# In-place products in tiles of two states, and one accumulating transfer for two of them, in a state-space recurrence

## The chip, the cores and the metric

The kernel runs on 1 core of one Trainium2 chip. The metric is the time of one execution on the device in microseconds (us). Before the change it is 2311.16 us, the median of 3 runs (2310.63 to 2311.9).

The core's engines are named as in the profile: PE (TensorE's matmuls), PEld (its weight loads), DVE (VectorE), ACT (ScalarE), POOL (GpSimd) and SP (SyncE, which only issues transfers here). Each takes its own instructions in order; they wait for one another by semaphores.

## The reference, cut to what matters

A residual network of four layers on x of 4 batches x 1024 positions x 128 features, all in float32. Each layer has a sequence mixer and a feed-forward part. The change lies in the mixer of the last layer, a selective state-space recurrence over 256 channels with 16 states each:

```python
xs = silu(conv(x @ in_w.T) + conv_b)
delta = softplus(xs @ wd1.T @ wd2.T + wd2_b)
Bm, Cm = xs @ wb.T, xs @ wc.T                 # 16 values per position
def step(h, inp):
    d_l, b_l, c_l, x_l = inp
    h = jnp.exp(d_l[:, :, None] * A) * h + (d_l * x_l)[:, :, None] * b_l[:, None, :]
    y_l = jnp.einsum('ben,bn->be', h, c_l)
    return (h, y_l)
y = (ys + xs * W_D) * silu(skip) @ out_w.T
```

The feed-forward part behind it has 8 experts with 512 hidden units, each computed for every position and weighted by a gate.

## The kernel before, in words

The last layer (`l3`, L1600) works in eight halves: 4 batches, each in two halves of 512 positions. The second half of a batch (h = 1) goes on from the states at the end of the first (h = 0). The 256 channels lie as two groups of 128 partitions, so a tile of one state is 128 x 2 x 512 floats.

`l3_scan` (L1824) is a generator that yields once per state n, 16 times a half. For one state:

- SP loads row n of B and of C, broadcast to all partitions, into `bn` and `cn` (L1849, four buffers each).
- POOL multiplies `ud` (delta times x) by B into a tile `db` (L1854, four buffers).
- For each channel group, ACT takes the exponential `da` of delta times A into one of two PSUM banks (L1858), and DVE runs the recurrence along the positions with one scan, in place in `db` (L1859).
- If h is 0, ACT copies the last position of both groups, 128 x 2 elements, to `carry` (L1868), from which the scans of the second half start.
- POOL multiplies `db` by C into a tile `hc` (L1870, four buffers).
- The sum over the states is PE's: `add` (L1836) multiplies an `hc` tile by the identity, once per channel group, and accumulates in two PSUM banks, `pys`. A list `sums` holds what is still to be summed: (state, tile, the state at which it is due).
- In batches 1 to 3, after each odd state, POOL issues a transfer that adds the odd state's `hc` to the even state's (L1875, `accum_op`), so that PE sums one tile for two states. The last state of the last half is left out of this.

`l3` advances one state of the scan, one step of the sum and finish of the half before (`l3_sum` L1884, `l3_finish` L1909: gate, output product, norm, router) and one step of the preparation of the next half (`l3_prepare` L1723), all under a raised priority (L1624); then come steps of the second mixture-of-experts layer (`moe`) and three or four steps of `work`, the experts of the last layer (`l3_experts` L1647, `l3_ffn` L1967). The experts take up a half when more than three states have passed since its router (L1655, L1637). Each expert has four matmuls `ph` (L1983) with a Relu on ACT (L1985), 16 matmuls `py` (L1993), and DVE adds them to `h_acc` under the gate (L2010).

The order on each engine is not the order of the source: a scheduler (`schedule_with_timeline_sim`, L2221) plans the program with its own costs, takes the instruction with the highest priority among those that are ready by its plan, and gives out tile buffers as they come free in it. The order is then fixed.

Of the kernel before, what the change touches and what calls it, by code (L numbers as in the profile page):

```python
# [12 lines left out]
F32 = mybir.dt.float32  # L13
# [3 lines left out]
ALU = mybir.AluOpType  # L17
# [3 lines left out]
P = 128  # L21
# [21 lines left out]
E3, NST, DDELTA, KCONV = 256, 16, 64, 4  # L43
# [17 lines left out]
class Net:  # L61
# [1762 lines left out]
    def l3_scan(self, u):  # L1824


        nc, c3, b, h = self.nc, self.c3, u["b"], u["h"]
        sp, wp, aneg = c3["sp"], c3["wp"], c3["aneg"]
        wout = c3["we"][:, :, ND:]
        xnT, xs, dl, ud, rows = (u[k] for k in ("xnT", "xs", "dl", "ud", "rows"))  # L1830
        carry = wp.tile([P, 2, NST], F32, name="carry") if h == 0 else u["prev"]["carry"]
        u["carry"] = carry
        u["py"] = py = []
        u["sums"] = sums = []

        def add(n, hc):  # L1836
            if not py:
                py.extend(self.psb(f"y{ec}", [P, 512], f"pys{ec}") for ec in range(2))
                u["first"] = n
            for ec in range(2):  # L1840
                self.mm(py[ec], self.ident, hc[:, ec, :], n == u["first"], n == NST - 1)

        u["add"] = add
        for n in range(NST):
            bc = []
            for i, nm in enumerate(("bn", "cn")):
                t = wp.tile([P, 1, 512], F32, name=nm, bufs=4)
                r = i * NST + n
                nc.sync.dma_start(  # L1849
                    out=t[:, 0, :], in_=rows[r : r + 1, :].to_broadcast([P, 512])  # L1850
                )
                bc.append(t.to_broadcast([P, 2, 512]))
            db = wp.tile([P, 2, 512], F32, name="db", bufs=4)
            nc.gpsimd.tensor_mul(db, ud, bc[0])  # L1854
            for ec in range(2):
                j = ec * NST + n
                da = self.psb("da", [P, 512], "da")
                nc.scalar.activation(da, dl[:, ec, :], AF.Exp, scale=aneg[:, j : j + 1])  # L1858
                nc.vector.tensor_tensor_scan(  # L1859
                    db[:, ec, :],  # L1860
                    da,
                    db[:, ec, :],
                    carry[:, ec, n : n + 1] if h else 0.0,
                    ALU.mult,
                    ALU.add,
                )
            if h == 0:
                nc.scalar.copy(carry[:, :, n : n + 1], db[:, :, 511:512])  # L1868
            hc = wp.tile([P, 2, 512], F32, name="hc", bufs=4)
            nc.gpsimd.tensor_mul(hc, db, bc[1])  # L1870
            if n in (9, 12):
                self.l3_gate(u, n // 12)
            if n % 2 and b > 0 and not (u["final"] and n == NST - 1):
                hc0 = sums.pop()[1]
                nc.gpsimd.dma_start(out=hc0, in_=hc, accum_op=ALU.add)  # L1875
                sums.append((n, hc0, n + 2))
            else:
                sums.append((n, hc, n + 2))
            for k in range(2):
                if sums and sums[0][2] <= n:  # L1880
                    add(*sums.pop(0)[0:2])
            yield
# [342 lines left out]
```

## Time and profile before

| What | Value |
|---|---|
| median of 3 runs | 2311.16 us |
| the profiled execution's own time | 2313.25 us |
| its span | 2311.5 us |
| mean granted TensorE clock | 0.928 |
| busy share of the span: PE, DVE, ACT, POOL | 87%, 59%, 52%, 44% |
| recurrence, from its first product with B to its last sum | about 1388 to 2181 us |
| products with B (L1854): of 128, 112 under the name `ud`, mean | 2642 ns |
| products with C (L1870), 128, mean | 2499 ns |
| accumulating transfers (L1875) | 47, of 512 KB |
| matmul records of the sums (`pys`) | 324, busy 158.1 us |
| carry copies on ACT (L1868) | 64, median 194 ns |

A busy share is an average over stages. The answer by stage gives the busy time of each engine in a stretch, then the granted clock, the mean share of the 16 transfer engines in use, and GB/s. A group of instructions is read as: line, engine, operation, result<-inputs, shapes, count | busy us, mean ns of one | idle time of the engine just before them, and what ended most of it. A mean over products on POOL is longer than the 2.35 us of one alone, as a product behind an issue of a transfer is recorded from before that issue's end. A wait is read as: who waited <- for whom: us in total, times, the longest. In the timeline, "x2" is two instructions merged into one line.

### The profile page before, as it was taken

To read this page: it belongs to the slowest core of one execution; us is meant where nothing else is said; L and a number is where in the kernel's file an instruction comes from. 1 tells how busy PE (TensorE), PEld (TensorE's weight loads), DVE (VectorE), ACT (ScalarE), POOL (GpSimd) and SP (SyncE) were. 2 spreads that over 40 slices of the span, in tenths; PEclk is the share of its full clock that TensorE was granted. 3 is DMA by queue.
4 is the path that set the end of the run, shared out by engine and by line. 5 is a ranking of instruction groups with operands and counts; after the bars stand their busy time and mean duration, and the time that the engine had idled before them with its cause. 6 is when DMAs were issued, how large, how long until landed. Compare 5 with 4: busy or idle time off the path is not lost.

```text
span 2311.5 us, 46328 instructions
## 1 busy us (share of the span) xinstructions
PE 2004.4 (87%) x17788; PEld 1398.0 (60%) x17788; DVE 1355.3 (59%) x3674; ACT 1193.8 (52%) x2609; POOL 1023.8 (44%) x812
## 2 busy tenths in 40 slices
PE   6679789989999999999979865688898999898998
PEld 3455565544477777787768653346565656565666
DVE  7658544343455654654645555785777688777522
ACT  6532334322244444454555546476767786766443
POOL 5100410000123244234143337987788889888500
PEclk9768879989999999999989987899999999999999
DMA  3000110050000010031222065455775677775421
GB/s 106 0 28 10 40 38 1 19 172 0 1 3 2 3 38 22 25 89 42 77 75 79 22 203 165 123 176 169 210 220 158 172 190 198 189 190 164 117 64 51
DMA packets 138603, 211.09 MB, mean 91 GB/s; under 512 B 18644, under 2 KB 75981, under 8 KB 137998
## 3 DMA queue, kind: packets, MB, share of 16 engines
q1 hardware_dynamic: 126238, 173.87, 24.6%
q0 software_dynamic: 12144, 34.26, 7.2%
q8 instruction: 140, 2.29, 0.4%
q14 instruction: 81, 0.66, 0.1%
HBM read 160.29 MB, written 23.16 MB: 79 GB/s over the span
## 4 chain that ended last, share of the span: by engine, by line
PE 44%; DVE 12%; ACT 11%; issue 4%; another core or an unknown queue 1%; POOL 1%; DMA 1%; DVEq 0%; ACTq 0%; SPq 0%; POOLq 0%
PE py L129 8%; PE ph L129 7%; PE po L1131 5%; PE pa_m L129 5%; PE pqk L129 5%; DVE db L1859 4%; PE kp_mo L129 3%; PE pys L129 2%; PE pv L129 2%; PE pr L1201 2%; ACT da L1858 1%; PE pt L133 1%; ACT hh L1985 1%; PE kp_mo L133 1%; ACT xN L176 1%
## 5 line engine op out<-in xcount | busy, mean ns | idle before, releaser
L1064 POOL TENSOR_TENSOR qt<-r_q,sb_c_turn 128x256 f32<-128x256 f32 (+1 forms) x256 | 164.4, 662 | 455.8 <-ACT r_q L1056 451.6
L1870 POOL TENSOR_TENSOR hc<-db,cn 128x1024 f32<-128x1024 f32 x128 | 315.6, 2499 | 85.0 <-PE pys L129 34.6
L129 PEld LDWEIGHTS py<-wh,hh 128*128 128x128 f32 x2048 | 254.4, 195 | 84.4 <-issue 48.2
L1854 POOL TENSOR_TENSOR db<-ud,bn 128x1024 f32<-128x1024 f32 x112 | 288.3, 2642 | 12.7 <-issue 10.2
L129 PE MATMUL ph<-xT,wh 128*128 128x512 f32 x512 | 259.4, 624 | 26.3 <-DVE h_acc L2010 8.3
L129 PE MATMUL py<-wh,hh 128*128 128x128 f32 x2048 | 261.8, 279 | 17.0 <-ACT hh L1985 7.8
L1985 ACT ACTIVATE hh<-ph,sb_cols 128x512 f32<-128x512 f32 x256 | 170.6, 681 | 134.8 <-PE ph L129 102.1
L1122 DVE TENSOR_TENSOR a<-pa_m,sb_c_near 128x256 f32<-128x256 f32 x256 | 96.7, 419 | 210.6 <-PE pa_m L129 198.1
L1079 ACT ACTIVATE kN<-kp_mo,sb_c_trig 128x128 f32<-128x128 f32 x448 | 129.8, 371 | 131.3 <-PE kp_mo L133 122.9
L1858 ACT ACTIVATE da<-dl,aneg 128x512 f32<-128x512 f32 x224 | 153.3, 689 | 79.9 <-DVE db L1859 76.5
L129 PE MATMUL pys<-hc,sb_c_ident 128*128 128x512 f32 x324 | 158.1, 618 | 18.3 <-POOL hc L1870 15.1
L1859 DVE TENSOR_TENSOR_SCAN db<-da,carry,db 128x512 f32<-128x512 f32 x128 | 157.2, 1267 | 12.4 <-ACT da L1858 9.4
L129 PEld LDWEIGHTS ph<-xT,wh 128*128 128x128 f32 x512 | 90.3, 198 | 109.3 <-issue 55.5
L1859 DVE TENSOR_TENSOR_SCAN db<-da,db 128x512 f32<-128x512 f32 x128 | 149.5, 1206 | 9.2 <-POOL db L1854 5.2
L2010 DVE SCALAR_TENSOR_TENSOR h_acc<-py,gt,h_acc 128x128 f32<-128x128 f32 x252 | 70.9, 343 | 134.2 <-PE py L129 132.2
L129 PE MATMUL pqk<-xT,wE 128*128 128x256 f32 x512 | 136.3, 389 | 8.4 <-ACT coT L1198 4.3
L129 PEld LDWEIGHTS pys<-hc,sb_c_ident 128*128 128x128 f32 x324 | 60.7, 199 | 80.5 <-issue 57.7
L129 PEld LDWEIGHTS pqk<-xT,wE 128*128 128x128 f32 x512 | 88.6, 193 | 21.8 <-DVE cv L1041 6.6
L1198 ACT COPY coT<-pt 128x512 f32<-128x512 f32 x64 | 37.5, 586 | 117.1 <-PE pt L133 117.1
L129 PE MATMUL po<-ht,wD 128*128 128x512 f32 x192 | 93.1, 597 | 0.0
L1131 PE MATMUL po<-cv,a 128*64 128x65 f32 x2048 | 89.2, 230 | 0.0
L844 DVE TENSOR_SCALAR ht<-ph,sb_cols 128x512 f32<-128x512 f32 x48 | 35.7, 749 | 90.8 <-PE ph L129 90.6
(454 smaller groups left out, 4297.4 us busy)
## 6 DMA issues: line engine op xcount, KB each, us to landing
wx<-in_wF SPq DMA_DIRECT2D x92, 384.0 KB
bn<-rows SPq DMA_DIRECT2D x128, 256.0 KB
cn<-rows SPq DMA_DIRECT2D x128, 256.0 KB
wh<-in_wH SPq DMA_DIRECT2D x64, 512.0 KB
hc<-hc POOLq DMA_DIRECT2D x47, 512.0 KB
xrows<-zero SPq DMA_DIRECT2D x4, 1472.0 KB
xg<-xrows SPq DMA_DIRECT2D x20, 256.0 KB
yrows<-ys SPq DMA_DIRECT2D x20, 256.0 KB
```

The costliest lines, as they stand in the source:

```text
L129: return self.nc.tensor.matmul(out=out, lhsT=lhsT, rhs=rhs, start=start, stop=stop)
L133: self.nc.tensor.transpose(out, in_, self.ident[0:n, 0:n])
L1064: nc.gpsimd.tensor_mul(u["qt"][:, m, a:], u["q"][:, a:], c2["turn"][:, m, o + a : o + 2 * P])
L1079: self.nc.scalar.activation(u["kN"][:, c, m, :], pk[:, c, :], AF.Copy, scale=trig[:, k, m : m + 1])
L1122: nc.vector.tensor_mul(u["a"][:, i, :, :], pa[i], self.c2["near"][:, None, :].to_broadcast([P, 2, P]),)
L1131: self.nc.tensor.matmul(out=u["po"][self.HALF[j], i, c, :], lhsT=lhsT, rhs=rhs, start=key not in u["begun"], stop=True, skip_group_check=True,
L1854: nc.gpsimd.tensor_mul(db, ud, bc[0])
L1858: nc.scalar.activation(da, dl[:, ec, :], AF.Exp, scale=aneg[:, j : j + 1])
L1859: nc.vector.tensor_tensor_scan(db[:, ec, :], da, db[:, ec, :], carry[:, ec, n : n + 1] if h else 0.0, ALU.mult, ALU.add,)
L1870: nc.gpsimd.tensor_mul(hc, db, bc[1])
L1985: nc.scalar.activation(ht, ph, AF.Relu, bias=self.col("h_b1", i=e * NK + k))
L2010: nc.vector.scalar_tensor_tensor(acc[:, c, :], py[:, c, :], gt[:, c, e : e + 1], acc[:, c, :], ALU.mult, ALU.add,)
```

## The change

`db` becomes a view of one half of a tile `pair` that holds two states, and there are four such tiles. The product with C is taken in place in `db`, and the `hc` tiles are gone. The carry is copied by DVE instead of ACT. In batches 1 to 3, after every fourth state one transfer adds the tile of states 4q+2 and 4q+3 to the tile of 4q and 4q+1; the two sums are due three states after it. In batch 0, and for the last four states of the last half, every state is summed by itself.

```diff
-            db = wp.tile([P, 2, 512], F32, name="db", bufs=4)
+            if n % 2 == 0:
+                pair = wp.tile([P, 2, 2, 512], F32, name="db", bufs=4)
+                if n % 4 == 0:
+                    base = pair
+            db = pair[:, n % 2, :, :]
             nc.gpsimd.tensor_mul(db, ud, bc[0])
...
             if h == 0:
-                nc.scalar.copy(carry[:, :, n : n + 1], db[:, :, 511:512])
-            hc = wp.tile([P, 2, 512], F32, name="hc", bufs=4)
-            nc.gpsimd.tensor_mul(hc, db, bc[1])
+                nc.vector.tensor_copy(carry[:, :, n : n + 1], db[:, :, 511:512])
+            nc.gpsimd.tensor_mul(db, db, bc[1])
             if n in (9, 12):
                 self.l3_gate(u, n // 12)
-            if n % 2 and b > 0 and not (u["final"] and n == NST - 1):
-                hc0 = sums.pop()[1]
-                nc.gpsimd.dma_start(out=hc0, in_=hc, accum_op=ALU.add)
-                sums.append((n, hc0, n + 2))
-            else:
-                sums.append((n, hc, n + 2))
+            if b == 0 or (u["final"] and n >= NST - 4):
+                sums.append((n, db, n + 2))
+            elif n % 4 == 3:
+                nc.gpsimd.dma_start(out=base, in_=pair, accum_op=ALU.add)
+                sums.extend((n - 1 + k, base[:, k, :, :], n + 3) for k in range(2))
```

## The prediction

> **What bounds the kernel now.** I read the page first, its shares by engine and its list of groups, then busy time by stage, then the waits of the recurrence stage, then the timeline around single instructions.
>
> ```profile
> PE 2004.4 (87%) x17788; PEld 1398.0 (60%) x17788; DVE 1355.3 (59%) x3674; ACT 1193.8 (52%) x2609; POOL 1023.8 (44%) x812
> ...
> L1870 POOL TENSOR_TENSOR hc<-db,cn 128x1024 f32<-128x1024 f32 x128 | 315.6, 2499 | 85.0 <-PE pys L129 34.6
> ```
>
> POOL's 44% is an average over stages with different limits. By halves of the recurrence (columns: stretch, length, busy PE, PEld, DVE, ACT, POOL, clock) it is another engine:
>
> ```profile
> 1600.00:1699.00 99.00, 82.35 (x451) 58.21 (x452) 73.59 (x146) 72.10 (x148) 84.22 (x43) 0.98 0.73 202
> ...
> 1815.00:1907.00 92.00, 85.54 (x413) 53.85 (x411) 75.71 (x147) 77.36 (x144) 81.13 (x41) 1.00 0.71 189
> 1907.00:1996.00 89.00, 81.94 (x403) 52.60 (x403) 72.22 (x131) 63.18 (x106) 80.71 (x41) 1.00 0.71 192
> 1996.00:2093.00 97.00, 90.50 (x422) 57.12 (x420) 74.09 (x139) 66.86 (x115) 81.47 (x41) 0.97 0.68 181
> ```
>
> PE is busy for 92 to 93% of three of these halves, POOL for 84 to 91%, DVE for 74 to 82%. Four quantities close together: whichever engine gets some 15 us more per half becomes the bound. The waits between 1600 and 2185 us say who is late (waiter, releaser, us, times, longest):
>
> ```profile
> DVE h_acc L2010 <- PE py L129: 48.2, 21, 6.4
> ...
> POOL hc L1870 <- PE pys L129: 34.6, 13, 5.0
> ...
> PE ph L129 <- DVE h_acc L2010: 8.3, 9, 2.9
> ...
> PE pys L129 <- DMA hc<-hc: 3.3, 4, 1.2
> ```
>
> POOL waits for PE, to get an hc buffer back; PE waits for DVE, and hardly for a transfer. In 585 us PE is busy 531.6, so all that any change off PE can give here is the 53 us that are left.
>
> **The change, part by part.**
>
> *Transfers.* 47 become 23 (four per half instead of eight in batches 1 to 3, three in the last half). On POOL an issue holds back the next product: at 1829.79 one is issued and the next product starts at 1830.38, 0.59 us later, and the pair and issue up to 1835.00 take 5.21 us against 4.66 for two products. I call it 0.6 us. If one of 1 MB costs the same, POOL gets back 24 x 0.6 = 14 us over 550 us; if it costs double, 0.4 us. I take 14 us of POOL's time. POOL is not the fullest engine, so a third of it, **-5 us**; ends 0 and -14.
> Landing: the issue at 2068.81 released PE at 2079.49, that at 2073.13 at 2082.72, so 10.7 and 9.6 us. The page gives the software queue 7.2% of 16 engines' span for 34.26 MB: 0.072 x 2311.5 / 34.26 = 4.9 us per MB, so 2.5 us more per transfer of 1 MB; landing after 12 to 13 us. Inside a half a sum is due three states after its transfer instead of two, 17 us at 5.7 us a state: hidden. At the end of a half PE may come too early by these 2.5 us: 5 ends, 0 to +12.5; it waited 3.3 us in all so far, and one transfer stands there instead of two. I take **0**.
> The row says that PE waited 3.3 us for 47 transfers. The Trainium skill, page "DMA: Bandwidth & Descriptors", section "Anatomy of one DMA", gives each transfer about 2.0 us of fixed cost; by that rule 24 transfers fewer would be worth 48 us, were they on the path, and by the row at most 3.3. I go by the row.
>
> *In place.* Each product has the same shape, so 2.33 to 2.36 us as now. The hc buffers go; db tiles hold eight states in the bytes that held four and four. In batch 0 POOL can thus run further ahead; between 1385 and 1490 it idled 9.9 us for DVE's scans and 1.9 on issue. Ends 0 and -11.8, and I take **-3**, as most of that waits for scans, not for buffers. Later, POOL's 34.6 us of waiting for PE lose their cause, but a POOL that waits for PE is not the bound: 0, except for the last product of all, which waited 4.82 us at 2166 and starts the final chain: **-2** (ends 0 and -5). A db tile is now held until PE has summed it, so a late PE holds up a product with B, 2.35 us ahead of a scan, where it held up a product with C; with eight states that is due two states early. I take 0.
>
> *Sums.* 162 products with the identity become 164: 64 in batch 0, 5 x 16, and 20 in the last half. The trace has two records each at 0.43 us pitch: four records, **+1.7 us** of PE. They come two at a time; at the end of a half the second moves one state (5.7 us) later, and with it gate and norm. The experts take a half over only after more than three states, and that covers it; without the cover it is an idle PE of up to 5.7 us, five times: 0 to +28. I take 0.
>
> *Carry.* 64 copies of 128x2 leave ACT (0.19 us each, 12 us of 1194; its 11.0 us of waiting before them moves to the next exponential, which needs the same scan: 0) and go to DVE. Without company that is 64 x 0.17 = 11 us. But here is the row that decides. One line of the kernel, L1294, copies from SBUF to SBUF on DVE in 2 or 4 elements; it takes 0.17 us, except beside POOL (DVE, then POOL):
>
> ```profile
> 1156.89 0.25 DVE L1294 COPY tend<-tend 128x2 f32<-128x2 f32 x1
> 1157.05 0.15 DVE L1295 TENSOR_TENSOR tend<-tend 128x6 f32<-128x6 f32 x1
> 1157.23 0.59 DVE L1294 COPY tend<-tend 128x4 f32<-128x4 f32 x1
> ```
>
> ```profile
> 1156.37 1.42 POOL L1064 TENSOR_TENSOR qt<-r_q,sb_c_turn 128x256 f32<-128x256 f32 x2 [3.86 <-ACT r_q L1056]
> ```
>
> POOL's two products end at about 1157.08 and 1157.79; the copies end at 1157.14 and 1157.82. Each waited until POOL's running instruction was over. The scans do not: all 128 that start a batch take 1.19 to 1.22 us, most of them beside POOL. So the carry's copy, right behind a scan on DVE's queue, should wait for the rest of a 2.35 us product: POOL is busy 0.85 of the time, half a product is left on average, 0.85 x 1.17 = 1.0 us, and 0.17 for itself. Sixteen copies give 19 us in each half that starts a batch. Ends: 0 (all in DVE's slack), and 64 x (2.35 + 0.17) = 161 us. I take the mean, since DVE has slack: its 73.6, 75.7 and 74.1 us in the first halves of batches 1 to 3 become 92.6, 94.7 and 93.1. None of the four halves above is fuller than 93% on any engine, so at that share these last 99.6, 101.8 and 100.1 us, against 99, 92 and 97: +13. At 90%, two engines being full now, 102.9, 105.2 and 103.4: +23. Batch 0's has 59.5 of 98 us and can take it. I take **+18**. Behind the copy wait the next scans, and for them ACT's exponentials (two banks) and so its Relus, and PE. POOL's product with C now waits for the copy as well, but that is over at POOL's own border; behind it waits the next product with B. 0 to +0.2 us per copy, in POOL's slack.
>
> The rows show two copies held. The Trainium skill, page "SBUF — State Buffer", section "Who interferes with whom", says that a copy on VectorE that uses both ports and a GpSimd instruction exclude each other for the whole instruction, whichever starts first; it speaks against moving the copy. By it POOL too could lose 64 x 0.17 = 11 us (estimate), which the rows do not show; with that the sum would be at most 11 us higher.
>
> **Sum:** -5 - 3 - 2 + 1.7 + 18 = +9.7 us on the profiled execution's 2313.25 us (span 2311.5 and 1.75 around it), so 2323. That execution lies 2.1 us above the median of the runs, 2311.16; as a median I say **2321**.
>
> **Rivals.**
> 1. *Faster: the buffers were the limit.* POOL's chain paces the half (products, issue, landing, buffer back), the trace's quads of 21.8 us hold 19.9 us of POOL work, and with fewer issues and no wait for PE each of 22 quads loses 0.6 and part of 1.5 us. For it: 34.6 us of waits in 13 places. Against it: PE is full in just these quads (21.80 of 21.80 us from 1827.5). A fifth to a third of PE's 53 idle us: -11 to -18, and +1.7 for the sums: 2295 to 2302. It decides if the copies find POOL between two products, so that they cost less than 0.3 us each.
> 2. *Nothing:* the copies fit DVE's slack, POOL's gain lies behind PE: 2311 to 2314, with +1.7 from the sums.
> 3. *Slower by the transfers:* PE, in order, stands before the last sums of each half for the longer landing, and the gate comes one state later: +12.5 to +28, 2324 to 2339. For it: at 2079.49 and 2082.72 PE did stand. Against it: 1.6 us in all there.
> 4. *It doesn't do what it says:* a transfer of 1 MB is issued at twice the cost, and POOL saves nothing: the forecast without -5, 2326.
>
> **How the numbers follow.** Forecast 0.44 (with rival 4), transfers 0.10, faster 0.28, nothing 0.18. What a measurement can tell from no change is 0.2%, 4.6 us. The forecast's own range is 2307 (copies +13, POOL's whole 14 gained) to 2336 (copies +23, no gain), so 0.40 of it is slower and 0.04 within; the transfers are slower; of the faster rival 0.26 is faster and 0.02 within; of nothing 0.14 is within and 0.02 on each side. Faster 0.28, same 0.20, slower 0.52. The range over all cases is 2295, rival 1's far end, to 2348, the forecast's 2336 with 12.5 for the landings. It leaves out a gain beyond a third of PE's idle time and the copies' bound of 161 us, 2 in 10.
>
> **What would show it.** Right: the copy's group on DVE has a mean near 1.2 us, DVE's busy time in the first halves of batches 1 to 3 rises to over 90 us, these halves get longer by 1 to 13 us, and those in between don't. Wrong: a mean below 0.3 us; then rival 1 or 2. The issue's 0.6 us is read behind the 23 transfers, the landing in PE's wait for them, and the buffers in POOL's waits for PE, which must be gone from the products with C. A new wait of the products with B for PE would show that the held tiles bite.

## The result, and the profile after

The changed kernel takes **2406.7 us** (median of 4 runs, 2400.6 to 2413.0) against 2311.5 us of the kernel before on the same chip: a ratio of 1.0398, 95% interval 1.0375 to 1.0420. It is slower by 4%, 95 us; 2321 had been forecast and 2348 was the upper end. The profiled execution has a span of 2398.8 us, 87 us more than before, at a mean granted clock of 0.912 instead of 0.928. The page's line of busy time, and the groups that replace that of the product with C:

```profile
PE 2043.1 (85%) x17792; PEld 1414.6 (59%) x17792; DVE 1426.2 (59%) x3738; ACT 1191.4 (50%) x2545; POOL 1003.1 (42%) x788
...
L1873 POOL TENSOR_TENSOR db<-db,cn 128x1024 f32<-128x1024 f32 x128 | 302.2, 2373 | 105.1 <-DVE carry L1872 37.0
```

The carry's copy stands only in the full list of groups (count | busy us, mean ns):

```profile
L1872 DVE COPY carry<-db 128x2 f32<-128x2 f32 x64 | 74.6, 1165 | 1.0
```

PE has four matmul records more, and 39 us more busy time: apart from these four, the same matmuls at a lower clock. POOL is less busy than before. The four halves that the prediction showed, cut in the same way (from one half's first product with C to the next's; columns as there):

```profile
1594.00:1714.00 120.00, 96.28 (x475) 66.93 (x474) 93.40 (x168) 79.27 (x149) 81.40 (x43) 0.90 0.65 181
1839.00:1953.00 114.00, 92.76 (x422) 57.53 (x422) 90.56 (x163) 77.15 (x129) 78.58 (x38) 0.90 0.55 150
1953.00:2055.00 102.00, 89.12 (x399) 55.93 (x398) 73.53 (x136) 66.97 (x110) 76.92 (x36) 0.93 0.63 166
2055.00:2167.00 112.00, 93.59 (x404) 57.84 (x403) 83.75 (x146) 63.49 (x98) 78.48 (x38) 0.89 0.56 156
```

They were 99, 92, 89 and 97 us. The three that start a batch are longer by 21, 22 and 15 us, and their DVE is busier by 10 to 20 us; but the one in between, which copies no carry, is longer by 13 us as well. So two things happened. And no engine is full: PE has gone from 83-93% down to 80-87%, DVE stands at 72 to 79%. The waits from 1600 to 2250 us:

```profile
POOL db L1873 <- DVE carry L1872: 36.7, 10, 13.1
POOL db L1858 <- DVE ud L1818: 31.2, 3, 15.7
...
POOL db L1858 <- DMA db<-db: 22.4, 6, 4.7
...
PE ph L129 <- DVE h_acc L2012: 15.1, 9, 4.0
...
PE pys L129 <- DMA db<-db: 7.1, 4, 3.2
```

POOL's waits for PE to get a buffer back, 34.6 us before, are gone. In their place it waits for the carry's copy (the product with C now overwrites what the copy reads; but e2 below, where it overwrites nothing, has 19.1 us of this wait too), for `ud` of the next half, and for the joining transfer to give back a tile. PE waits for DVE's `h_acc` nearly twice as long as before (8.3 us).

How long one copy can be held is seen where the longest starts, on DVE and then on POOL:

```profile
1609.53 0.41 DVE L1496 SCALAR_TENSOR_TENSOR sg<-sg,ph 128x256 f32<-128x256 f32 x1
1609.86 8.30 DVE L1872 COPY carry<-db 128x2 f32<-128x2 f32 x1
1618.08 0.41 DVE L1499 SCALAR_TENSOR_TENSOR mh<-sg,ph 128x256 f32<-128x256 f32 x1
```

```profile
1608.89 2.37 POOL L1873 TENSOR_TENSOR db<-db,cn 128x1024 f32<-128x1024 f32 x1
1611.21 2.34 POOL L1858 TENSOR_TENSOR db<-ud,bn 128x1024 f32<-128x1024 f32 x1
1613.51 2.34 POOL L1873 TENSOR_TENSOR db<-db,cn 128x1024 f32<-128x1024 f32 x1
1615.80 2.33 POOL L1858 TENSOR_TENSOR db<-ud,bn 128x1024 f32<-128x1024 f32 x1
1618.30 2.35 POOL L1873 TENSOR_TENSOR db<-db,cn 128x1024 f32<-128x1024 f32 x1 [0.17 <-POOL db L1858]
```

Four products follow on one another without a gap, and the copy ends at 1618.17 in the first gap between two (1618.13 to 1618.30). Of the 64 copies 25 took less than 0.2 us; each of the other 39 ended within 0.04 us of the end of a product on POOL.

What stands behind this copy on DVE's queue is what PE and ACT wait for:

```profile
1618.55 3.78 PE L129 MATMUL po<-sb_s_e,xs 128*128 128x128 f32 x16 [8.37 <-DVE mh L1499]
```

```profile
1619.66 0.69 ACT L1862 ACTIVATE da<-dl,aneg 128x512 f32<-128x512 f32 x1 [7.75 <-DVE db L1863]
```

PE sat idle for 8.37 us until `mh`, the instruction right behind the copy, and ACT for 7.75 us until the scan behind that.

### The profile page after: what moved, and what is told of

Read it like the earlier page. It is cut to its first block, busy times and chain, and to the rows that moved or that the text cites. A ratio compares the mean times of both kernels' runs of the same rounds, so it can differ in the third digit from the quotient of the medians.

```text
span 2398.8 us, 46140 instructions
## 1 busy us (share of the span) xinstructions
PE 2043.1 (85%) x17792; PEld 1414.6 (59%) x17792; DVE 1426.2 (59%) x3738; ACT 1191.4 (50%) x2545; POOL 1003.1 (42%) x788
## 5 line engine op out<-in xcount | busy, mean ns | idle before, releaser
L1873 POOL TENSOR_TENSOR db<-db,cn 128x1024 f32<-128x1024 f32 x128 | 302.2, 2373 | 105.1 <-DVE carry L1872 37.0
L129 PE MATMUL ph<-xT,wh 128*128 128x512 f32 x512 | 269.6, 642 | 49.7 <-DVE h_acc L2012 15.1
L1858 POOL TENSOR_TENSOR db<-ud,bn 128x1024 f32<-128x1024 f32 x112 | 262.5, 2363 | 71.9 <-DVE ud L1818 31.2
L129 PE MATMUL pys<-db,sb_c_ident 128*128 128x512 f32 x328 | 165.6, 645 | 26.6 <-POOL db L1873 16.3
L129 PEld LDWEIGHTS pys<-db,sb_c_ident 128*128 128x128 f32 x328 | 63.7, 206 | 99.9 <-issue 69.7
```

What stands on the lines that cost most here:

```text
L129: return self.nc.tensor.matmul(out=out, lhsT=lhsT, rhs=rhs, start=start, stop=stop)
L1873: nc.gpsimd.tensor_mul(db, db, bc[1])
```

## The experiments

Ratios are to runs of the kernel before on the same chip, with 95% intervals.

### The two parts, one at a time

**e1**: the changed kernel, carry back on ACT.

```diff
-                nc.vector.tensor_copy(carry[:, :, n : n + 1], db[:, :, 511:512])
+                nc.scalar.copy(carry[:, :, n : n + 1], db[:, :, 511:512])
```

> The changed kernel with the 64 carry copies back on ACT; nothing else differs in the source, and nothing is left out. Changed kernel 2406.7 us, kernel before 2311.5 us. Theory 1, the copies on DVE are the loss (in the trace of the changed kernel their mean is 1.17 us, and they end with POOL's instructions): 2305 to 2325 us, and PE's busy share in the six halves of batches 1 to 3 goes back from 85% to over 90%. Theory 2, the tiles are the loss (a db tile is held by the join and by PE's sums, and POOL's products with B no longer run ahead): over 2380 us, with the gaps on POOL ahead of the first product of a half as long as in the changed kernel. In between, by both: 2340 to 2370.

Measured 2350.8 us, ratio 1.0153 (1.0132 to 1.0175): in between. With the copies off DVE 56 us of the 95 are gone, and some 35 to 40 us are something else.

**e2**: the kernel before with that edit the other way round, DVE instead of ACT.

> The kernel before with one edit: the 64 carry copies on DVE. Theory 1, the copies alone are the loss: 2385 to 2410 us, with a mean copy of over 1 us. Theory 2, the tiles are the loss: 2311 to 2330 us, although the copies are as long. Both needed together: 2330 to 2350, with the first halves of batches 1 to 3 longer by some 10 us each.

2379.2 us, 1.0271 (1.0254 to 1.0288). The copies alone cost 63 us, a little under theory 1's 2385, and need nothing else of the change.

**e3**: the changed kernel with the same bytes in copies of one element.

```diff
-                nc.vector.tensor_copy(carry[:, :, n : n + 1], db[:, :, 511:512])
+                for ec in range(2):
+                    nc.vector.tensor_copy(carry[:, ec, n : n + 1], db[:, ec, 511:512])
```

> The changed kernel with each carry copy split into two DVE copies of one element per partition, one per channel group (128 instead of 64). If the copy is held by POOL only in the form that takes several elements, the mean falls from 1.17 us to about 0.16 and by theory 1 the time to 2310 to 2330 us. If any copy from SBUF to SBUF on DVE is held, the mean stays over 0.8 us, there are twice as many, and the time is 2406 or more. By theory 2 the time stays at 2380 to 2410 whatever the copies take.

```profile
L1873 DVE COPY carry<-db 128x1 f32<-128x1 f32 x128 | 15.7, 141 | 0.0
```

2356.0 us, 1.0179 (1.0146 to 1.0213). Twice as many copies take a fifth of the time: none of the 128 is held, though 91 of them run wholly inside a product on POOL. The time falls by 51 us, to about that of e1, and not to theory 1's 2310 to 2330, as the other part remains. The Trainium skill, page "VectorE: DVE Perf Modes", section "Mode 2×_2P — use both read ports for one tensor", lets a copy from SBUF to SBUF use both read ports if its outermost dimension above one is even: two elements qualify, and one element has no such dimension. That fits 1165 against 141 ns; no run here shows the ports themselves.

**e13**: the same edit as in e3 on the kernel before.

> The kernel before with the carry copied on DVE in two copies of one element per partition, 128 in all. If POOL's hold on the copy of two elements is the whole price of the 63 us: 2308 to 2325 us, with a mean copy of 0.14 us. If the move to DVE by itself, with the other order that it gives, costs a good part: 2335 to 2375.

2318.5 us, 1.0017 (1.0001 to 1.0033). Here the hold is nearly the whole price: 1.0271 with it, 1.0017 without. That another planned order made the difference can be ruled out from the traces. The copies left aside, POOL's 812 instructions follow one another in the same order in e2 and e13 (by the names of their tiles), and 3634 of DVE's 3674 and 17772 of PE's 17788 stand at the same place. For e3 and the changed kernel it is 768 of 788, 3524 of 3674 and 17614 of 17792.

The halves that start batches 1, 2 and 3, and third the one between the last two, in e13 and then in e2, cut where the last product with C ends:

```profile
1599.00:1705.00 106.00, 89.09 (x464) 60.58 (x463) 78.44 (x178) 75.34 (x142) 87.07 (x47) 0.97 0.69 193
1816.00:1913.00 97.00, 88.43 (x436) 57.15 (x435) 76.08 (x176) 74.69 (x127) 81.99 (x42) 0.98 0.67 180
1913.00:2003.00 90.00, 81.92 (x387) 51.84 (x387) 72.65 (x135) 66.02 (x110) 81.59 (x41) 0.98 0.71 191
2003.00:2093.00 90.00, 86.02 (x433) 56.71 (x432) 71.02 (x160) 62.72 (x99) 81.73 (x41) 1.00 0.73 194
```

```profile
1596.00:1721.00 125.00, 94.60 (x449) 63.78 (x448) 103.75 (x162) 74.51 (x140) 86.73 (x47) 0.89 0.59 165
1838.00:1954.00 116.00, 97.32 (x435) 62.02 (x434) 94.44 (x158) 73.94 (x124) 81.27 (x40) 0.91 0.56 150
1954.00:2044.00 90.00, 81.89 (x378) 51.44 (x378) 73.30 (x136) 66.41 (x110) 81.07 (x40) 0.96 0.71 190
2044.00:2149.00 105.00, 90.37 (x431) 58.16 (x431) 88.87 (x144) 62.78 (x99) 82.38 (x42) 0.97 0.63 167
```

The halves with copies are longer by 19, 19 and 15 us, the one without by nothing; the half in between that is not shown, of batch 1, is longer by 5. DVE is busier by 25, 18 and 18 us, and most of its idle time stays: 27.6, 20.9 and 19.0 us in e13, 21.3, 21.6 and 16.1 in e2. So the copies took little of DVE's slack; most of them was added to the length. Of batch 2's 19 us, 10 are idle PE (8.6 becomes 18.7 us) and 9 are nearly the same number of matmuls at a granted clock of 0.91 instead of 0.98. In batches 1 and 3 idle PE has more of it: 13.5 us against 5.5, and 10.7 against 4.4.

### What the tiles and the join cost

**e4**: the kernel before with the products in place alone.

```diff
-            db = wp.tile([P, 2, 512], F32, name="db", bufs=4)
+            db = wp.tile([P, 2, 512], F32, name="db", bufs=8)
...
-            hc = wp.tile([P, 2, 512], F32, name="hc", bufs=4)
-            nc.gpsimd.tensor_mul(hc, db, bc[1])
+            hc = db
+            nc.gpsimd.tensor_mul(db, db, bc[1])
```

> The kernel before with the products with C taken in place alone: db tiles of one state, eight of them, no hc tiles; carry on ACT, 47 transfers of 512 KB as before. Theory 2 in the form that holding db tiles until PE's sum costs: 2340 us or more, with POOL's products with B waiting for PE or for a transfer. Theory 2 in the form that only tiles of two states and joins over four states cost: 2300 to 2320. Theory 1: 2300 to 2315, as eight tiles in one pool let POOL run further ahead.

2333.1 us, 1.0088 (1.0056 to 1.0119): between the two forms. POOL runs on, up to eight states, and then stands at the border of the half (e4, waits from 1600 us on):

```profile
POOL db L1854 <- DVE ud L1818: 69.3, 5, 21.6
```

It was 2.5 us in the kernel before. What POOL gains inside a half it seems to lose at its end, waiting for the preparation of the next.

**e5** and **e6** asked whether that preparation paces everything: a second `next(nxt, None)` per state, in the kernel before and in e1's.

> The kernel before with one edit: two steps of the next half's preparation per state instead of one; nothing is left out. In the kernel before the first product with B of the last three halves starts 0 to 1 us after the last ud of its preparation (92, 90 and 98 us after the half's own first product). Theory A, the preparation paces the halves of every one of these kernels: ud is ready earlier, and the time falls to 2270 to 2300 us. Theory B, PE paces the kernel before (93% busy), and ud is late only because it stands in PE's order: 2305 to 2320, or slower, as the preparation is then pressed in between the sums.

> The changed kernel with the carry on ACT (2350.8 us) and two steps of the preparation per state. In it POOL waited 46 us for ud at the borders of the halves. Theory A, the in-place tiles cost time because POOL stands at the border until the preparation is over: these waits shrink to under 20 us and the time to 2300 to 2330. Theory B, it is the sums, bunched behind the joins, that hold PE up, and the wait for ud is what is left over: 2340 to 2360, with the wait only moved to another place.

2350.5 us (1.0150, 1.0118 to 1.0181) and 2373.2 (1.0257, 1.0227 to 1.0287): both slower by 22 us or more. Theory A falls: an earlier preparation does not make these kernels faster. That it pushes other work back is likely, and not shown.

**e7**: e1 with each join issued as two transfers of 512 KB.

```diff
-                nc.gpsimd.dma_start(out=base, in_=pair, accum_op=ALU.add)
+                for k in range(2):
+                    nc.gpsimd.dma_start(
+                        out=base[:, k, :, :], in_=pair[:, k, :, :], accum_op=ALU.add
+                    )
```

> The changed kernel with the carry on ACT (2350.8 us) and each joining transfer of 1 MB issued as two of 512 KB, one per state, in the same place. If the number or the size of the transfers matters by itself (one issue of 0.6 us more on POOL for each of 23; a landing that is 2 us shorter), the time moves by 5 to 15 us, up by the issues or down by the landings. If only the distance of the join matters (four states are held until the fourth product), it stays at 2346 to 2356.

2353.8 us, 1.0171 (1.0139 to 1.0203), not apart from e1: half as many transfers of twice the bytes gain nothing that can be measured.

**e8** and **e12**: e4 with six and with five tiles instead of eight (`bufs=6`, `bufs=5`).

> The kernel with in place alone (single tiles, carry on ACT, 47 transfers, 2333.1 us) with six db tiles instead of eight; the rest is as it was. If what costs is that products with B wait for tiles that PE's sums still hold, fewer tiles make it worse: 2345 to 2400. If what costs is that POOL runs too far ahead with products with B and so delays the products with C, the joins and the sums (the first sums of a half come 41 us into it instead of 32 to 36), fewer tiles make it better: 2310 to 2328.

> In place with five single tiles, carry on ACT, 47 transfers (eight tiles 2333.1 us, six 2309.2). Theory C, the fewer the better until scans wait for tiles: 2300 to 2315. Theory D, with five the products with B wait for the transfers and for PE's sums: 2325 to 2400.

2309.2 us, 0.9973 (0.9955 to 0.9991), and 2326.9, 1.0043 (1.0025 to 1.0061). With six tiles the wait for `ud` is back at 3.5 us. It is the one version ahead of both kernels, and of the kernel before by some 6 us. I took it to show that running ahead does the harm (theory C), until **e16**, with seven:

> In place with seven single tiles, carry on ACT, 47 transfers (five 2326.9 us, six 2309.2, eight 2333.1). If the time follows from how far POOL runs ahead, smoothly: 2312 to 2328. If it is the planned order that changes by chance with every edit, by some 10 to 20 us, anything from 2300 to 2345 can come, and the difference of six and eight tiles is no effect of the number.

2354.2 us, 1.0186 (1.0155 to 1.0216), the slowest of the series. Five, six, seven and eight tiles give 1.0043, 0.9973, 1.0186 and 1.0088: no order. Theory C falls too. Each edit gives the scheduler another plan (only 549 of POOL's 812 instructions stand at the same place in e4 and in e8), and the time seems to move by 1 to 2% with it; whether six tiles are a better size or a lucky plan is not told apart here.

**e9**: e1 with three tiles of two states.

> The changed kernel with the carry on ACT (2350.8 us) and three tiles of two states instead of four. Six tiles of one state had been 24 us better than eight (2309.2 against 2333.1). Theory C, eight states in flight let POOL run ahead with products with B and bunch the sums: here too it gets better, 2315 to 2340 us. Theory D, the join over four states needs its tiles (a base is held from its first product until PE's sums three states after the join, so with three tiles only one is left to go on with): worse, 2365 to 2450, with POOL's products with B waiting for PE and for the transfer.

2383.4 us, 1.0284 (1.0242 to 1.0327). Here the wait is plain:

```profile
POOL db L1858 <- DMA db<-db: 155.2, 22, 10.7
```

**e10**: e1's tiles with the join of the kernel before, 512 KB from the odd into the even half of one tile, due two states later.

```diff
-            if b == 0 or (u["final"] and n >= NST - 4):
-                sums.append((n, db, n + 2))
-            elif n % 4 == 3:
-                nc.gpsimd.dma_start(out=base, in_=pair, accum_op=ALU.add)
-                sums.extend((n - 1 + k, base[:, k, :, :], n + 3) for k in range(2))
+            if n % 2 and b > 0 and not (u["final"] and n == NST - 1):
+                hc0 = sums.pop()[1]
+                nc.gpsimd.dma_start(out=hc0, in_=db, accum_op=ALU.add)
+                sums.append((n, hc0, n + 2))
+            else:
+                sums.append((n, db, n + 2))
```

> The changed kernel with the carry on ACT (2350.8 us), its four tiles of two states kept, but the join of the kernel before: after each odd state 512 KB are added from the odd to the even half of the same tile (47 transfers), summed two states later. Single tiles with the same joins gave 2333.1 us. If what makes the 18 us between those two is the join over four states, this goes to 2325 to 2340; if it is that a tile of two states is given back as a whole, it stays at 2345 to 2365.

2326.2 us, 1.0047 (1.0027 to 1.0067): by these two runs the join over four states costs 25 us, the tiles of two states little or nothing.

**e14**: the other way round, e4's eight single tiles with the join over four, two transfers of 512 KB.

> In place in eight single tiles with the carry on ACT, joined over four states by two transfers of 512 KB after every fourth state (state 4q+2 into 4q, 4q+3 into 4q+1), sums three states later. Joined in neighbours it was 2333.1 us, and with tiles of two states and this join 2353.8. If the join over four states costs by itself, wherever the tiles end: 2345 to 2365. If it costs only because a tile of two states comes back as a whole: 2325 to 2340.

2351.1 us, 1.0165 (1.0140 to 1.0191), with the join at e1's and e7's place again.

**e15**: e1 with the last four states of each half joined in neighbours.

> The changed kernel with the carry on ACT (2350.8 us), but the last four states of each half of batches 1 to 3 joined in neighbours (odd into even, due two states later), the others over four as before; in the last half the last four are summed one by one, as they were. If the 25 us of the join over four arise at the ends of the halves (the last sums come later, and the gate, the norm and the experts behind them): 2322 to 2338. If they arise where the ninth state waits for its tile (4 to 10 us each time, once or twice a half): 2340 to 2355.

2351.1 us, 1.0173 (1.0147 to 1.0199): nothing is won by earlier sums at the end of a half. The second expectation gives the time to the ninth state's wait for its tile. There is such a wait, seen in e1 on POOL:

```profile
1843.89 0.86 POOL L1879 DMA_DIRECT2D db<-db  x1
1845.86 2.35 POOL L1873 TENSOR_TENSOR db<-db,cn 128x1024 f32<-128x1024 f32 x1 [1.11 <-DMA cn<-rows]
1848.53 0.92 POOL L1879 DMA_DIRECT2D db<-db  x1 [0.31 <-POOL db L1873]
1853.97 4.66 POOL L1858 TENSOR_TENSOR db<-ud,bn 128x1024 f32<-128x1024 f32 x2 [4.52 <-DMA db<-db]
1861.70 4.67 POOL L1858 TENSOR_TENSOR db<-ud,bn 128x1024 f32<-128x1024 f32 x2 [3.08 <-DMA db<-db]
```

The first join is issued at 1843.89, and the product with B of state 8 starts 10.1 us later; the second at 1848.53, and that of state 10 starts 13.2 us later. In the stretch of e1 from 1600 to 2200 us POOL waited so ten times, 38.3 us. But other traces do not let this wait be the cause. The same wait in e14 and in e12, from 1600 us on:

```profile
POOL db L1854 <- DMA db<-db: 1.7, 1, 1.7
```

```profile
POOL db L1854 <- DMA db<-db: 43.0, 21, 7.6
```

e14 hardly waits and is as slow as e1; e12, with joins in neighbours, waits longer than e1 and has 1.0043. So the step from "the join over four costs 25 us" to "because a tile comes back late" is not shown. Another wait, of POOL for the row of C (`cn`), was not followed up: there is none in the kernel before from 1600 us on, and it is 13.3 us in e1, 23.9 in e14, 37.8 in e7 and 41.0 in the changed kernel, but also 21.3 in e4 and 17.3 in e10, which are faster.

### The copies a third time

**e11**: e8 (six tiles) with the carry on DVE. **e17**: the same in copies of one element.

> In place with six single tiles (2309.2 us), with the 64 carry copies on DVE. On the kernel before this edit cost 63 us, on the changed kernel 56. If the copies cost some 60 us in any order of the work: 2360 to 2380. If the price hangs on how far POOL runs ahead (POOL busy behind more scans), it is under 40 here: 2330 to 2350.

> In place with six single tiles, the carry copied on DVE in two copies of one element each. Carry on ACT gave 2309.2 us, copies of two elements on DVE 2341.7. If the 32 us between them are POOL's hold on the copies: 2305 to 2320. If they come from the planned order that the move to DVE brings: 2330 to 2350.

2341.7 us, 1.0128 (1.0078 to 1.0177); and 2291.1 us on a faster chip, where the kernel before took 2278.7, so 1.0058 (1.0032 to 1.0083). Against e8's 0.9973 that is 1.5% for the copies, of which the hold makes about 0.7% (0.1 to 1.3% by the two intervals), and the other 0.85% stays when it is gone. On e11's chip 1.0058 would be about 2330 us, the lower end of the second expectation. The copies are held here as well (60.6 us in all), but with six tiles the price seems to be a third of that on the other two kernels. This pair is less clean than e2 and e13: 720 of POOL's 812 instructions and 3198 of DVE's 3674 stand at the same place. What stays, 0.85%, is more than the 0.2 to 0.3% that moving the copies to DVE cost without the hold there (e13 against the kernel before, e3 against e1); that it is another plan is likely, and not shown.

## Why the prediction was wrong

*Carry.* That the copy waits on DVE while POOL multiplies was right. The mean of 1.17 us that was worked out, against 1.165 measured, was luck: the prediction let each copy wait at most for the rest of one product, 85% of them for half of it. In fact 39 of 64 were held, for 1.8 us on average, and two of these for 7.3 and 8.3 us. In e2 the same copies took 89 us, mean 1.40, and 50 us of these belong to the ten that took longer than the 2.52 us that the prediction set as the most for one. DVE's busy time rose to 93.4 and 90.6 us and, in batch 3, to only 83.8, where 92.6 to 94.7 was said.

**The step that failed is the next one**, "I take the mean, since DVE has slack ... None of the four halves above is fuller than 93% on any engine, so at that share these last 99.6, 101.8 and 100.1 us". That prices a delay by the fullness of its engine: +18. In e2 and e13 the hold cost 2.5%, 59 us, two thirds of the copies' 89 us, with DVE 81 to 85% busy; on the changed kernel (e3) 51 us of 75. DVE's slack did not take the copies up: a copy stands in front of the `mh`, the scan and the `h_acc` that PE and ACT wait for, as the copy at 1609.86 shows (8.37 us of idle PE, 7.75 of idle ACT). And the longer busy time of PE at a lower granted clock, not in the sum at all, made 4 to 9 us of the 15 to 19 in each half. The forecast for the halves in between, no change from the copies, held for batches 2 and 3, and was 5 us short for batch 1.

*In place.* Transfers, buffers and sums together were put at -8 us; what e1 and e3 leave of the loss is 35 to 41 us. So "with eight states that is due two states early. I take 0" failed, with the gains of -3 and -2; how much of the 35 to 41 us belongs to it is open. The sign that the prediction named, a new wait of the products with B for PE, did not come in the changed kernel; they wait for `ud` (31.2 us) and for the joining transfer (22.4 us) instead. The join over four holds two of the four tiles until the fourth product, and then for a landing of 10 us. In four versions with that join (e1, e7, e14, e15) the ratios are 1.0153 to 1.0173; with eight states of tiles and joins in neighbours they are 1.0047 and 1.0088 (e10, e4). That is some 15 to 29 us. But seven tiles without it gave 1.0186, so I cannot separate it cleanly from the plan, and e14, with 1.7 us of the wait for the tile, shows that this wait does not carry it. What in place alone costs stays open: -6 to +43 us by the number of tiles, in no order.

*Transfers.* A 1 MB issue costs what was taken: the next product starts 0.65 us behind the one at 1798.95 in the changed kernel. So rival 4 is wrong. (At double cost its saving would be 47 x 0.6 - 23 x 1.2 = 0.6 us, not 0.4; nothing hangs on it.) -5 was too much: e7 against e1 shows nothing. The landing of 12 to 13 us was about right (10 to 13), and PE's waits for it stayed small (7.1 us): it was hidden from PE, but POOL now waits for it to get a tile. Rival 3 looked at the ends of the halves, and e15 gives no sign that they matter.

*Sums.* Four records more, as said.

*Rival 1* held that POOL's wait for PE was worth something: it did vanish, and came back as a wait for `ud` or for a tile.

*The range* left out the copies' full price, "the copies' bound of 161 us". With its own 75 us for the copies, the honest upper end was all of it on the path, 2386, and the tiles on top.

## What to carry to other kernels

A small instruction that another engine can hold is priced first by its whole held time, put in front of what stands behind it on its queue, and not by how full its engine is: a gap on an engine that waits for others is not room. Here two thirds of the held time reached the total on two kernels, and about a quarter on the one with six tiles. Ask of an edit that saves buffers who gives the tile back, and after which landing: with three tiles of two states (e9) POOL waited 155 us for it. Where a scheduler plans the order anew for every edit, change one thing in several ways before believing a difference of 1%: here four tile counts gave a spread of 2%. And compare the order of the instructions in two traces: where it is the same, as in e2 and e13, the plan is no rival.

## What the runs showed of the hardware

- A copy of 128x2 from SBUF to SBUF on DVE is held while POOL multiplies, and not just for the product that is running: 8.30 us in the changed kernel, 10.26 us in e2. A copy of 128x1 is never held (0.14 us, 256 of them in e3 and e13), nor is a scan that reads one operand from PSUM (at most 1.29 us in these kernels). The Trainium skill, page "SBUF — State Buffer", section "Who interferes with whom", says that the loser of the shared port pair blocks for the whole instruction; the runs add that it can lose several turns in a row.
- More idle time on PE and a lower granted clock came together: in e2's three halves with copies, against e13's, PE idles 10 to 14 us more, and the clock is 0.89, 0.91 and 0.97 instead of 0.97, 0.98 and 1.00. In batch 2's, 435 matmuls took 97.3 us where 436 had taken 88.4. The share of idle time alone does not set the clock: PE is 83% busy at 0.98 in the first half that the prediction shows, and 84% busy at 0.91 in e2.
